# Two layers of attention and experts on one core: the second norm's factors spread by DMA

## The chip, the core and the metric

One core of a Trainium2 chip runs the whole program. Its engines run side by side and meet only at semaphores: TensorE (PE, with weight loads shown apart as PEld), VectorE (DVE), ScalarE (ACT), GpSimd (POOL), and SyncE (SP), whose queue issues nearly all transfers here. The metric is the device time of one execution in microseconds. A run's time is the median of several executions; the profile is of one execution.

## The reference

Two transformer layers on x of 16 x 256 tokens with 128 features, all in float32. Each layer adds to x an attention and a mixture of experts, both of a norm of x. What matters here is that the attention norms once more what was already normed:

```
xn = layernorm(x)                       # outer norm, no weights
x  = x + attention(xn, ln_w, ln_b, ...) + experts(xn, ...)

# inside the attention of either layer:
mu, var = mean(xn), mean((xn - mu)**2)
xh = (xn - mu) * rsqrt(var + 1e-5) * ln_w + ln_b
```

Since xn has mean 0, the second norm is a factor per token, r2 = (var(xn) + 1e-5)**-0.5, then a weight and a bias per feature. Layer 0 has 8-head local attention with rotary positions and 8 experts (2 per token); layer 1 has a gated attention unit and 32 experts (8 per token).

## The kernel before

**Tiling.** The 4096 tokens are cut into NG = 8 groups of G = 512. A group's rows lie as 128 partitions x 4 chunks x 128 features (token c*128 + p is at partition p, chunk c). Matmuls want features on the partitions, so rows are turned: `transposed` (L175) takes a PSUM bank and turns the four chunks by PE against `ident`. Turned tiles are 128 features x 512 tokens.

**Norms.** `moments` (L141) and `normalise` (L155) make xn on DVE, with a power on POOL; `again` (L163) makes r2, 128 x 4 (one factor per token), its last step a power on POOL (L169). Then there are two turned forms of each group: `xnT` of the rows xn themselves, for the routing and the experts, copied out of PSUM by ACT; and `xhT`, for the attention. For the latter `scaled` (L171) multiplies the four chunks by r2 on DVE (L173), `transposed` turns them on PE (L179), and one ACT activation takes the bank to SBUF with the weight as scale and the bias as bias, both one value per partition (L363 in layer 0, L794 in layer 1).

**Layer 0's attention** (L506 to L621) is a loop over s from -3 to 64, one step per pair of heads and sequence, eight steps a group; a step takes about 5 us. The order of PE, DVE, ACT and POOL is written out by hand (`manual_schedule`, L506). In one step, in this order: PE turns the softmax of step s (`turned0`, L465); ACT copies it out (L472) and takes the exponentials of step s + 2 (L442); DVE divides three quarters of step s + 1 (L451); then come pieces of other groups' routing (`pieces`), and the steps of `prepare` (L357); DVE multiplies what `there` holds (L407); PE and DVE make the scores of step s + 3 (L426, L432); ACT divides the last quarter of step s + 1 (L456), up to s + 1 = 48; PE attends (L482). `prepare(g)` has two parts: the scaling, in the step that `turned_rows` names, and the turn with the activation, at the first step of the group before (s = 8(g - 1)). Its result `xhTs` is read by `rotated` (L386, from the next step on) and `values` (L370). `rotated` also has ACT copy a tile to `here` and SP move it in four transfers to `there` (L399), 32 partitions over.

SP's queue is not in the hand-written order. The framework's scheduler places its instructions at build time; so the transfers that zero `x_rows` (L615), written one every second step, stand in the trace in bunches of nine.

**The experts of layer 0** (L706 to L735) follow, untouched by the change.

**Layer 1** (L950 to L994): after a written start only POOL's order is by hand; PE, DVE, ACT and SP are ordered by the scheduler. For each group the loop runs 17 pairs of expert matmuls (`pair`, L937, L939, L974) and, between them, the attention of this group (`gau`), the expert choice of the next (`route1`, from L798; its weights `w` are turned on PE at L186 as `wT_ps`, stored by SP at L194, and spread over the partitions as `bc`, L842), and the preparation of the next group, `finish0` (L747), whose eight pieces end with the scaling (L790) and the turn with the activation (L792 to L795). `xhTs[g]` is read by `gau(g)`, which starts at the first pair of the next group.

Of the kernel before, what the change touches and what calls it, by code (L numbers as in the profile page):

```python
# [11 lines left out]
F32 = mybir.dt.float32  # L12
# [3 lines left out]
ALU = mybir.AluOpType  # L16
# [3 lines left out]
P = 128  # L20
B, N, D = 16, 256, 128
T = B * N
G = 512
NG = T // G
NC = G // P
# [22 lines left out]
def two_layers(ctx: ExitStack, tc: tile.TileContext, a: dict, out: bass.AP):  # L48
    nc = tc.nc
# [6 lines left out]
    rows = ctx.enter_context(tc.tile_pool(name="rows", bufs=2, space=bass.MemoryType.DRAM))  # L56
# [72 lines left out]
    xn_all = w_a.tile([P, NG * NC, D], F32, tag="xn_all", name="xn_all")  # L129
    r2_all = const.tile([P, NG, NC], F32, tag="r2_all", name="r2_all")  # L130
# [32 lines left out]
    def again(r2, var, rs, name):  # L163

        ve = small.tile([P, NC], F32, tag="bve2", name=f"bve2_{name}")
        nc.vector.tensor_tensor(ve, rs, rs, ALU.mult)
        nc.vector.tensor_tensor(ve, ve, var, ALU.mult)
        nc.vector.tensor_scalar(ve, ve, EPS, None, ALU.add)
        nc.gpsimd.tensor_tensor(r2, ve, mhalf, ALU.pow)  # L169

    def scaled(dst, src, r2):  # L171
        for c in range(NC):
            nc.vector.tensor_scalar(dst[:, c, :], src[:, c, :], r2[:, c : c + 1], None, ALU.mult)  # L173

    def transposed(src, name):  # L175

        t = mm_tile(name)
        for c in range(NC):
            nc.tensor.transpose(t[:, c * P : (c + 1) * P], src[:, c, :], ident)  # L179
        return t  # L180
# [155 lines left out]
    yTs, xnTs = [], []  # L336
    with first as pa:
        wk = pa.enter_context(tc.tile_pool(name="wkA", bufs=2))
# [16 lines left out]
        xhTs0, vs, oTs, heads, yps = {}, {}, {}, {}, {}  # L355

        def prepare(g):  # L357
            xh = wk.tile([P, NC, D], F32, tag="xh", name=f"xh_{g}")
            scaled(xh, xn_all[:, g * NC : (g + 1) * NC, :], r2_all[:, g, :])
            yield  # L360
            t = transposed(xh, f"xhT_{g}")
            xhT = wk.tile([P, G], F32, tag="xhT", name=f"xhTs_{g}")
            nc.scalar.activation(xhT, t, AF.Identity, bias=col("ln_b"), scale=col("ln_g"))  # L363
            xhTs0[g] = xhT
            vs[g] = wk.tile([P, NC, 512], F32, tag="v", name=f"v_{g}")
            yield
# [139 lines left out]
        with tc.manual_schedule(engines={order.PE, order.DVE, order.Activation, order.Pool}):  # L506
            routing = {g: routed(g) for g in range(NG)}
            preparing = {g: prepare(g) for g in range(NG)}

            def step(gens, g, n=1):  # L510
                if 0 <= g < NG:
                    for _ in range(n):
                        next(gens[g], None)

            def drain(fs):
                for f in fs:
                    f()
                fs.clear()

            pieces = {}
            for g in range(NG):
                b = 5 * g - 12
                ranks = (b + 12, b + 13, b + 14)
                if g == 0:
                    at = (-3, -2, -1, 0, 1, 2)
                elif g == 1:
                    at = (-1, 0, 1, 2, 4, 5, 6)
                elif g == NG - 1:  # L530
                    at = (b, b + 1, b + 2, b + 3, b + 4, b + 5, b + 6, b + 9, b + 10, b + 11)
                else:
                    at = (b, b + 1, b + 2, b + 4, b + 6, b + 8, b + 9, *ranks)
                for n in at:
                    pieces.setdefault(n, []).append(g)
            turned_rows = {2: 7, 3: 12, 4: 22, 5: 27, 6: 37, 7: 47}

            step(routing, 0, 3)
            step(preparing, 0, 2)
            rotated(0)  # L540
            drain(later)
            rotated(1)
            near, far, sums = turning.pop(0)
            near()
            step(routing, 0)
            step(routing, 1, 3)
            far()
            sums()
            drain(later)
            wo, upper, steps, tiles, sw1, sw2, gtw, gtb, tieg = load_rest()  # L550
            turning[0].pop(0)()
            for s in range(-3, NS + 1):
                g, r = divmod(s, 8)
                if 0 <= s < NS:
                    tps = turned0(s, sc.pop(s)[0])
                drain(later)
                if 0 <= s < NS:
                    pTs[s] = evicted(s, tps)
                if 0 <= s + 2 < NS:
                    sms[s + 2] = exponentials(s + 2, *sc[s + 2])  # L560
                if turning and len(turning[0]) == 3:
                    turning[0].pop(0)()
                    far = sums = None
                else:
                    far, sums = turning.pop(0) if turning else (None, None)
                if 0 <= s + 1 < NS:
                    sm = sms.pop(s + 1)
                    divided(s + 1, sc[s + 1][0], sm)

                if s == -2:  # L570
                    step(preparing, 1)
                for n in pieces.get(s, ()):
                    step(routing, n)
                if r == 0:
                    step(preparing, g + 1)
                for n in turned_rows:
                    if turned_rows[n] == s:
                        step(preparing, n)
                if s == 35:
                    placing = places0(wk)  # L580
                if 35 <= s < 43:
                    next(placing)
                if far:
                    far()
                if s + 3 < NS:
                    sc[s + 3] = scores(s + 3)
                if sums:
                    sums()
                if 0 <= s + 1 < SHARED:
                    divided_last(sc[s + 1][0], sm)  # L590
                if s >= 1:
                    attended(s - 1, pTs.pop(s - 1))

                if s % 2 and 2 <= (s + 7) // 2 < NS // 2:
                    rotated((s + 7) // 2)
                if s < -1:
                    for c in range(2):
                        values(0, 2 * (s + 3) + c)
                if s < 0:
                    continue  # L600
                if 0 < g < NG and r in (0, 2):
                    project(g - 1, r // 2)
                if s == NS - 2:
                    project(NG - 1, 0)
                if r in (4, 6) and g + 1 < NG:
                    values(g + 1, r - 4)
                    values(g + 1, r - 3)
                if s == 2:
                    zero = w_a.tile([P, 2 * D], F32, tag="zero", name="zero")
                    nc.gpsimd.memset(zero, 0.0)  # L610
                    x_r0 = x_rows.rearrange("(t p c) d -> p t (c d)", p=P, c=2)

                if s >= 2 and s % 2 == 0 and s - 2 < NT0:
                    n = min(2, NT0 - (s - 2))
                    nc.sync.dma_start(  # L615
                        out=x_r0[:, s - 2 : s - 2 + n, :], in_=zero.unsqueeze(1).to_broadcast([P, n, 2 * D])
                    )
                if s >= 41:
                    for n in range(3 * (s - 41), min(3 * (s - 40), 2 * NG * NC)):
                        scatter0(n, paces[n % 3])  # L620
            project(NG - 1, 1)  # L621
# [21 lines left out]
    with ExitStack() as pb:  # L643
        wk = pb.enter_context(tc.tile_pool(name="wkB", bufs=2))
# [81 lines left out]
        for t in range(NT0 + at[-1]):  # L726
# [3 lines left out]
            if t % 3 == 0 and t // 3 < len(wanted):  # L730
                name, shape, src = wanted[t // 3]
# [11 lines left out]
    with ExitStack() as pc:  # L743
        wk = pc.enter_context(tc.tile_pool(name="wkC", bufs=2, reuse_waits="tile"))
        xn1Ts, xhTs, scs, spread_w = {}, {}, {}, {}

        def finish0(g):  # L747

            yg = wk.tile([P, NC * 2, D], F32, tag="yg", name=f"yg_{g}", bufs=1)
            for c in range(NC):  # L750
                for s in range(2):
                    nc.gpsimd.indirect_dma_start(  # L752
                        out=yg[:, 2 * c + s, :], out_offset=None, in_=y_rows,
# [6 lines left out]
            t = transposed(yTs[g].rearrange("p (c t) -> p c t", t=P), f"yt_{g}")  # L760
# [9 lines left out]
            xn = wk.tile([P, NC, D], F32, tag="xn", name=f"xn1_{g}")  # L770
            r2 = small.tile([P, NC], F32, tag="brs2", name=f"brs2_{g}")
            again(r2, *normalise(xn, xs[g], *moments(xs[g], f"c{g}")), f"d{g}")
            nc.gpsimd.tensor_tensor(xs[g], xs[g], xn, ALU.add)
            yield
            t = transposed(xn, f"xn1T_{g}")
            xnT = wk.tile([P, G], F32, tag="xn1T", name=f"xn1Ts_{g}")
            nc.scalar.copy(xnT, t)
# [7 lines left out]
            sc = wk.tile([P, NC, E1], F32, tag="sc", name=f"sc_{g}")  # L785
            nc.scalar.activation(sc.rearrange("p c e -> p (c e)"), gl[:, : NC * E1], AF.Sigmoid)
            scs[g] = sc
            yield
            xh = wk.tile([P, NC, D], F32, tag="xh", name=f"xh1_{g}")
            scaled(xh, xn, r2)  # L790
            yield
            t = transposed(xh, f"xh1T_{g}")  # L792
            xhT = wk.tile([P, G], F32, tag="xh1T", name=f"xh1Ts_{g}")
            nc.scalar.activation(xhT, t, AF.Identity, bias=col("ln_b1"), scale=col("ln_w1"))  # L794
            xhTs[g] = xhT  # L795
# [298 lines left out]
```

## Time and profile before

| what | value |
|---|---|
| median of 3 runs (lowest, highest) | 957.95 us (957.24, 962.34) |
| the profiled execution, whole | 944.71 us |
| its span, first to last instruction | 942.9 us |
| granted TensorE clock | 0.996 |
| layer 0's attention | to about 345 us |
| layer 0's experts | about 345 to 440 us |
| layer 1 | from about 440 us; one group 59.2 us |
| turns of the second norm on PE | 64, of which the change leaves 8 |

The span is that of one execution, on which all single durations were read; the median of the runs is 13 us above that execution's time. Busy time of an engine counts overlapped matmuls to their modelled end, so a full PE row says that PE is never without work, not that each listed nanosecond could be had back; the chain of work that ended last gives each instruction only the time that it adds. A line of the timeline has the start, the duration, the engine, the line, the operation, output and inputs with their shapes, a count of merged instructions, and in brackets the idle time before it and what ended it.

### The profile page before, as it was taken

What the parts mean: (1) busy time and instruction counts of PE and PEld (TensorE: products, weight loads), DVE (VectorE), ACT (ScalarE), POOL (GpSimd) and SP (SyncE); (2) the same over time, 40 slices, a digit from 0 to 9 for tenths busy, and PEclk for the clock granted to TensorE, in tenths of its full rate; (3) what the DMA queues carried; (4) which work ended last, traced back from release to release, by engine and by line L of the source; (5) the groups of instructions that cost most, each with busy time, mean ns of one, the idle gap of its engine ahead of it and who ended that gap; (6) DMA issues with size and microseconds to landing.
All of it is one profiled execution on the core that took longest, in us unless ns stands there. A gap on an engine that the chain in (4) does not pass through costs nothing.

```text
span 942.9 us, 13590 instructions
## 1 busy us (share of the span) xinstructions
PE 899.7 (95%) x3848; PEld 516.7 (55%) x3848; DVE 702.7 (75%) x2265; ACT 491.3 (52%) x1200; POOL 287.3 (30%) x251
## 2 busy tenths in 40 slices
PE   3899999999999998989999999999999999999997
PEld 2556666555555648986445454554545545455453
DVE  4999999899999923332687685886868868688653
ACT  1788989798798853434433422434224342243411
POOL 2343433323467630001525231252322522221200
PEclk9999999999999999999999999999999999999999
DMA  7171110010122137873161434214342243421430
GB/s 198 25 243 32 27 31 24 24 34 23 49 76 78 55 117 237 245 219 128 28 169 48 120 79 107 74 53 112 85 107 70 56 108 89 106 64 42 102 88 11
DMA packets 64922, 84.54 MB, mean 90 GB/s; under 512 B 10321, under 2 KB 40785, under 8 KB 64337
## 3 DMA queue, kind: packets, MB, share of 16 engines
q1 hardware_dynamic: 60320, 74.75, 29.5%
q0 software_dynamic: 4096, 8.40, 2.9%
q8 instruction: 31, 0.51, 0.2%
q10 hardware_dynamic: 432, 0.53, 0.2%
q14 instruction: 43, 0.34, 0.1%
HBM read 58.22 MB, written 17.04 MB: 80 GB/s over the span
## 4 chain that ended last, share of the span: by engine, by line
PE 63%; DVE 22%; DMA 6%; ACT 3%; issue 2%; SPq 2%; POOL 1%; DVEq 0%; ACTq 0%; POOLq 0%
PE u L939 11%; PE g L937 10%; PE z L974 9%; DVE p L432 4%; PE s L426 4%; PE o L482 3%; DVE p L451 3%; PE o L912 3%; DMA y_rows<-yt 3%; PE yr L696 2%; PE h L685 2%; PE t L465 2%; PE y L495 2%; PE z L992 2%; PE pq L386 2%
## 5 line engine op out<-in xcount | busy, mean ns | idle before, releaser
L941 ACT ACTIVATE h<-g 128x512 f32<-128x512 f32 x128 | 75.3, 594 | 232.0 <-PE g L937 225.6
L943 DVE TENSOR_TENSOR h<-h,u 128x512 f32<-128x512 f32 x128 | 87.2, 683 | 62.9 <-PE u L939 61.6
L937 PE MATMUL g<-xn1Ts,eg 128*128 128x512 f32 x256 | 131.4, 595 | 0.0
L939 PE MATMUL u<-xn1Ts,eu 128*128 128x512 f32 x256 | 130.2, 593 | 0.0
L442 ACT ACTIVATE p<-p,nm 128x256 f32<-128x256 f32 x256 | 127.5, 514 | 0.2 <-DVE nm L432 0.2
L974 PE MATMUL z<-h,ed 128*128 128x512 f32 x224 | 114.3, 593 | 0.0
L752 POOL DMA_INDIRECT yg<-y_rows,slot_at x64 | 69.8, 1090 | 121.4 <-PE hs L632 103.2
L432 DVE CUSTOM_DVE_ANT_0 p<-s,mask 128x256 f32<-128x256 f32 x256 | 92.7, 417 | 2.5 <-PE s L426 2.5
L946 DVE TENSOR_TENSOR h<-h,bc 128x512 f32<-128x512 f32 x128 | 90.2, 707 | 2.7
L426 PE MATMUL s<-k,q 64*128 64x256 f32 x512 | 84.5, 412 | 7.1 <-DVE k L411 4.3
L465 PEld LDWEIGHTS t<-ident,p 128*128 128x128 f32 x512 | 59.4, 140 | 35.0 <-issue 8.6
L322 POOL DMA_INDIRECT x_rows<-xn_all,slot_at x64 | 66.6, 1040 | 37.5 <-ACT pT L472 16.0
L939 PEld LDWEIGHTS u<-xn1Ts,eu 128*128 128x128 f32 x256 | 47.9, 192 | 54.4 <-issue 46.6
L472 ACT COPY pT<-t 128x512 f32<-128x512 f32 x128 | 69.2, 597 | 10.4 <-PE t L465 10.4
L974 PEld LDWEIGHTS z<-h,ed 128*128 128x128 f32 x224 | 42.4, 190 | 53.5 <-issue 45.6
L937 PEld LDWEIGHTS g<-xn1Ts,eg 128*128 128x128 f32 x256 | 46.3, 190 | 46.0 <-issue 41.1
L883 POOL TENSOR_TENSOR r1s<-r1s,sinr 128x512 f32<-128x512 f32 x16 | 23.5, 1468 | 156.9 <-ACT r1s L878 153.9
L482 PE MATMUL o<-pT,v 128*64 128x256 f32 x512 | 70.3, 396 | 0.3 <-ACT oT L487 0.2
L465 PE MATMUL t<-ident,p 128*128 128x128 f32 x512 | 67.3, 274 | 1.4 <-ACT p L456 1.4
L426 PEld LDWEIGHTS s<-k,q 64*128 64x128 f32 x512 | 51.2, 189 | 25.0 <-DVE nm L432 9.0
L451 DVE TENSOR_SCALAR p<-p,sm 128x256 f32<-128x256 f32 x208 | 62.0, 356 | 2.3
L688 ACT ACTIVATE h0s<-h,we 128x256 f32<-128x256 f32 x78 | 32.7, 470 | 57.6 <-issue 36.9
(252 smaller groups left out, 1541.3 us busy)
## 6 DMA issues: line engine op xcount, KB each, us to landing
bc<-rows_r SPq DMA_DIRECT2D x128, 256.0 KB, 4.2
there<-here SPq DMA_DIRECT2D x128, 64.0 KB, 2.0
we<-in_ex_dram SPq DMA_DIRECT2D x39, 129.0 KB, 3.2
xt<-x_rows SPq DMA_DIRECT2D x39, 128.0 KB, 3.2
y_rows<-yt SPq DMA_DIRECT2D x39, 128.0 KB, 3.0
x_rows<-zero SPq DMA_DIRECT2D x19, 256.0 KB, 3.3
x<-in_x_dram SPq DMA_DIRECT2D x8, 256.0 KB, 5.6
out_dram<-out SPq DMA_DIRECT2D x8, 256.0 KB, 2.6
```

What stands on the lines that cost most here:

```text
L426: nc.tensor.matmul(sp[h][:, i, :], q[rows, b, i * P : (i + 1) * P], k[rows, b, :], start=True, stop=True)
L432: nc.vector.tensor_tensor_reduce(out=pr[:, h, i, :], in0=sp[h][:, i, :], in1=mask[:, i, :], scale=-1.0, scalar=-NEG, op0=ALU.add, op1=ALU. ...
L442: paces[1] = nc.scalar.activation(row, row, AF.Exp, bias=nm[:, n : n + 1], scale=-1.0, accum_out=sm[:, n : n + 1])
L451: nc.vector.tensor_scalar(row, row, sm[:, n : n + 1], None, ALU.mult)
L465: nc.tensor.transpose(tp[:, at : at + P], pr[:, h, i, j * P : (j + 1) * P], ident)
L482: nc.tensor.matmul(op[h * DH : (h + 1) * DH, :], vs[g][:, 2 * b + j, (2 * hp + h) * DH : (2 * hp + h + 1) * DH], pT[:, h, j, :], start=(j ...
L937: nc.tensor.matmul(gp, wg, xn1Ts[g], start=True, stop=True)
L939: nc.tensor.matmul(up, wu, xn1Ts[g], start=True, stop=True)
L941: nc.scalar.activation(h, gp, AF.Silu)
L943: nc.vector.tensor_tensor(h, h, up, ALU.mult)
L946: nc.vector.tensor_tensor(h, h, spread_w[g][n // 2][:, n % 2, :], ALU.mult)
L974: nc.tensor.matmul(zp, w, r, start=(n == 1), stop=False)
```

## The change

In both layers the groups 1 to 7 no longer scale and turn the rows a second time. The factors r2 (128 x 4) are stored by SP to a row of 512 floats in DRAM (`row_stored`), and read back by SP onto all 128 partitions (`row_spread`, 128 x 512). DVE multiplies that tile in place by the turned rows that the routing has anyway (`xnTs[g]` in layer 0, `xnT` in layer 1), and the activation reads the product from SBUF. Group 0 stays as it was.

In layer 0 `prepare(g)` now has three parts. Store and spread come in the steps that `factors` names, the multiply and the activation where turn and activation were, at s = 8(g - 1). In layer 1 the store comes with the piece that turns xn, the spread with the routing scores, and the multiply with the activation in the last piece. The tile for the spread row takes the buffers of the scaled rows (tag `xh`, two of them).

```diff
+    def row_stored(r2, name):
+        d = rows.tile([1, G], F32, tag="row", name=f"row_{name}")
+        nc.sync.dma_start(out=d.rearrange("o (c p) -> p (o c)", p=P), in_=r2)
+        return d
+
+    def row_spread(d, pool, name):
+        t = pool.tile([P, G], F32, tag="xh", name=name)
+        nc.sync.dma_start(out=t, in_=d[0].partition_broadcast(P))
+        return t
...
         def prepare(g):
-            xh = wk.tile([P, NC, D], F32, tag="xh", name=f"xh_{g}")
-            scaled(xh, xn_all[:, g * NC : (g + 1) * NC, :], r2_all[:, g, :])
-            yield
-            t = transposed(xh, f"xhT_{g}")
+            if g:
+                d = row_stored(r2_all[:, g, :], f"a{g}")
+                yield
+                t = row_spread(d, wk, f"xh_{g}")
+                yield
+                nc.vector.tensor_tensor(t, t, xnTs[g], ALU.mult)
+            else:
+                xh = wk.tile([P, NC, D], F32, tag="xh", name=f"xh_{g}")
+                scaled(xh, xn_all[:, g * NC : (g + 1) * NC, :], r2_all[:, g, :])
+                yield
+                t = transposed(xh, f"xhT_{g}")
             xhT = wk.tile([P, G], F32, tag="xhT", name=f"xhTs_{g}")
             nc.scalar.activation(xhT, t, AF.Identity, bias=col("ln_b"), scale=col("ln_g"))
...
-            turned_rows = {2: 7, 3: 12, 4: 22, 5: 27, 6: 37, 7: 47}
+            factors = {1: (-3, -2), 2: (4, 6), 3: (10, 12), 4: (18, 20), 5: (27, 29), 6: (34, 36), 7: (43, 45)}
...
-                if s == -2:
-                    step(preparing, 1)
                 for n in pieces.get(s, ()):
                     step(routing, n)
                 if r == 0:
                     step(preparing, g + 1)
-                for n in turned_rows:
-                    if turned_rows[n] == s:
+                for n in factors:
+                    if s in factors[n]:
                         step(preparing, n)
...
         def finish0(g):
...
+            if g:
+                row = row_stored(r2, f"b{g}")
             t = transposed(xn, f"xn1T_{g}")
...
             scs[g] = sc
+            if g:
+                bc = row_spread(row, wk, f"xh1_{g}")
             yield
-            xh = wk.tile([P, NC, D], F32, tag="xh", name=f"xh1_{g}")
-            scaled(xh, xn, r2)
+            if not g:
+                xh = wk.tile([P, NC, D], F32, tag="xh", name=f"xh1_{g}")
+                scaled(xh, xn, r2)
             yield
-            t = transposed(xh, f"xh1T_{g}")
+            if g:
+                t = bc
+                nc.vector.tensor_tensor(t, t, xnT, ALU.mult)
+            else:
+                t = transposed(xh, f"xh1T_{g}")
             xhT = wk.tile([P, G], F32, tag="xh1T", name=f"xh1Ts_{g}")
             nc.scalar.activation(xhT, t, AF.Identity, bias=col("ln_b1"), scale=col("ln_w1"))
```

## Prediction, made before the changed kernel was run

> **What bounds the kernel now.** I read the page's busy line first, then the busy time by stage, then the chain of work that ended last, and last the timeline around the instructions that the change touches. The stages below are my cuts: two of layer 0's attention, one group of layer 1. Columns after the stretch: its length, then busy us and count of PE, PEld, DVE, ACT, POOL, then granted clock, DMA share, GB/s.
>
> ```profile
> PE 899.7 (95%) x3848; PEld 516.7 (55%) x3848; DVE 702.7 (75%) x2265; ACT 491.3 (52%) x1200; POOL 287.3 (30%) x251
> ...
> 67.00:121.00 54.00, 54.00 (x324) 33.26 (x325) 52.29 (x218) 48.72 (x150) 20.44 (x16) 1.00 0.15 38
> 229.00:320.00 91.00, 88.52 (x530) 52.08 (x528) 88.81 (x322) 77.88 (x241) 54.59 (x51) 1.00 0.22 63
> 579.00:638.00 59.00, 58.74 (x173) 29.89 (x172) 45.08 (x121) 21.04 (x32) 18.17 (x15) 1.00 0.34 86
> ```
>
> Two different machines are seen here. In layer 0's attention PE, DVE and ACT are all nearly full (97 to 100%, 97%, 86 to 90%), so whoever waits passes it on. In layer 1 PE alone is full and DVE has 14 us spare per group of 59. The chain says which engine sets the end where:
>
> ```profile
> 116.16 0.44 PE xhT L179 x4
> ...
> 148.88 0.78 DVE xh L173 x4
> ...
> 196.75 0.44 PE xhT L179 x4
> ```
> ```profile
> 565.35 0.44 PE xh1T L179 x4
> ```
>
> Going through the whole chain by time: DVE leads at 28 to 67, 126 to 167 and 236 to 320 us, PE leads at 67 to 121 and 167 to 229. In layer 1 it is PE, with one piece on DVE per group (567.6 to 572.8: the expert choice, which PE's turn of the weights `wT_ps` waits for). The page gives four turns 4 x 0.273 us busy, but the chain gives them 0.44: matmuls overlap, and 0.44 is what PE gets back.
>
> **What goes and what comes, per later group (7 in each layer).** Removed: four turns, 0.44 us of PE; four scalings of 128x128, 0.78 us of DVE. Added: one multiply 128x512 by 128x512. Its nearest row is the same shape from SBUF, `sq<-there,sinq`, 0.60 us from start to start (0.69 with its end). The activation reads SBUF instead of PSUM: 0.81 us (`r1s<-base`, 64x512, scale and bias) against 0.78, nothing. DVE thus gains 0.18 per group. Here a rule speaks against the change: the Trainium skill, "VectorE: DVE Perf Modes", section "Mode 2×_2P — use both read ports for one tensor", says that an f32 tensor-by-scalar handles two elements a cycle and a tensor-by-tensor one. At the page's 0.96 GHz, my estimate from it is 4 x 67 = 267 ns of streaming before and 533 after, a loss of 0.27 us a group, so 14 x 0.45 = 6.3 us more DVE work than by the rows. The rows decide, since each of the four short scalings takes 0.195 from start to start, far over 67 ns.
>
> **The two transfers.** The store writes 512 floats one by one to DRAM (partition p, column c goes to c*128+p); the spread reads 2 KB 128 times. Nearest rows:
>
> ```profile
> bc<-rows_r SPq DMA_DIRECT2D x128, 256.0 KB, 4.2
> rows_r<-wT SPq DMA_DIRECT2D x8, 64.0 KB, 1.6
> ```
>
> Spread: the same form as `bc`, 3.5 to 4.2 us, and `bc` go out in pairs, so I take 3.7. Store: the trace has no DRAM write of four-byte pieces. At least the 1.6 us of `rows_r`. Above, the Trainium skill, "DMA: Bandwidth & Descriptors": its rules for kernel authors say that a non-contiguous last dimension becomes one descriptor per element, and its section "Measured (HBM→SBUF, 128 partitions, SWDGE, issued from GpSimd)" gives some 10.5 ns a packet; 512 of these are an estimate of 5.4 us, 7.0 with the 1.6. No run here shows it. I take 2.3, near the row, since the pieces are spread over 16 engines. Factors to row: 2.3 + 0.1 + 3.7 = 6.1 us, at worst 11.2.
>
> Layer 0 covers that. Group 1 is tightest: its factors are ready at 20.7 and SP is free at 22.6, so the row lands at 28.7 (worst 33.8); the multiply stands at 41. For groups 2 to 7 four or more steps of 5 us lie between. On SP's queue stand the `there<-here` moves: in steady state the last of four lands some 2.5 us before `sq` reads it (130.7 against 133.16). Store and spread issue in about 0.45 us each, and SP can wait 2.3 between them: 3.2 at worst, once a group, so at most 0.7 us late. POOL's queue gets nothing new; SP's store waits for its power. Cost 0; without that cover up to 7 x 0.7 = 5 us.
>
> **What moves in layer 0: ACT now waits for DVE.** The scaling stood some steps ahead (s = 7, 12, 22, ...). The multiply stands in the step with s = 8k, behind that step's three divisions and a routing piece, and the activation in ACT's written order waits for it. PE's turn used to be done long before. Step 16 shows it:
>
> ```profile
> 118.22 0.88 DVE L451 TENSOR_SCALAR p<-p,sm 128x256 f32<-128x256 f32 x3
> 118.78 0.79 ACT L363 ACTIVATE xhTs<-xhT,vec 128x512 f32<-128x512 f32 x1
> 119.45 0.52 ACT L456 ACTIVATE p<-p,sm 128x256 f32<-128x256 f32 x1
> 120.25 0.19 DVE L231 TENSOR_TENSOR lg<-lg,rmx 128x32 f32<-128x32 f32 x1
> 120.36 0.42 DVE L432 CUSTOM_DVE_ANT_0 p<-s,mask 128x256 f32<-128x256 f32 x1
> 120.85 1.04 PE L465 MATMUL t<-ident,p 128*128 128x128 f32 x8
> 121.49 1.07 ACT L472 COPY pT<-t 128x512 f32<-128x512 f32 x2 [1.26 <-PE t L465]
> ```
>
> The multiply comes in at 120.36 and ends at 121.05; ACT stood ready at 118.78: a wait of 2.27. Behind it in ACT's queue is L456, which divides the last quarter of `p`, and PE's next eight turns (L465) wait for that quarter. The same reading for groups 1 to 7: multiply ends 41.99, 81.21, 121.05, 159.84, 201.45, 238.95, 280.26; ACT ready 40.17, 79.84, 118.78, 157.74, 199.38, 238.83, 278.69; waits 1.8, 1.4, 2.3, 2.1, 2.1, 0.1, 1.6, sum 11.4. Most is absorbed: ACT then idles 0.7 to 1.7 us for PE anyway (the 1.26 above), and where DVE leads it does not matter. Where PE leads, L456 now ends the turns later by more than the 0.44 saved: group 2, L456 ends 82.4 and the last three turns 82.8 against 82.2 (+0.6); group 3, 122.7 against 121.7, less 0.78 because DVE, almost never idle there, comes earlier by the removed scaling (+0.2); group 5, 203.1 against 201.9, less a 0.2 that PE waited anyway (+1.0). Where DVE leads: scalings out in groups 1, 4, 7 (-2.34), multiplies in 1, 4, 6, 7 (+2.40), and +0.2 in group 1, whose late ACT delays `here`. Layer 0: 0.6 + 0.2 + 1.0 + 0.06 + 0.2 = **+2.1 us**. Ends: -1.3 if ACT's wait costs nothing (3 x -0.44 + 0.06), about +10 if it is passed on in full (11.4 - 1.3).
>
> **Layer 1.** Here the framework's scheduler orders PE, DVE, ACT and SP; only POOL is written.
>
> ```profile
> 557.70 1.23 SPq L842 DMA_DIRECT2D bc<-rows_r  x2
> 557.83 1.01 POOL L169 TENSOR_TENSOR brs<-bve_d,mhalf 128x4 f32<-128x4 f32 x1 [2.66 <-DVE bve_d L168]
> 558.88 1.29 DVE L173 TENSOR_SCALAR xh<-xn,brs 128x128 f32<-128x128 f32 x1 [0.51 <-POOL brs L169]
> 567.61 0.69 DVE L943 TENSOR_TENSOR h<-h,u 128x512 f32<-128x512 f32 x1 [1.11 <-PE u L939]
> 572.89 0.61 PE L186 MATMUL wT_ps<-ident,w 128*32 128x128 f32 x4 [0.23 <-DVE w L834]
> ```
>
> Factors are ready at 558.84, and SP has issued its last `bc` by 558.93. The row lands at 558.9 + 6.1 = 565.0 (worst 570.1). DVE has a gap of 1.11 before 567.61, so a multiply at 565 to 567 is free and the group gains PE's 0.44. A multiply inside the expert choice delays `w` by 0.60 against 0.44 gained: +0.16. Nobody needs the activation before the next group begins, 20 us on. Between -0.44 and +0.16 I take -0.2, since the landing is nearer the gap: 7 x -0.2 = **-1.4 us** (ends -3.1 and +1.1). This rests on DVE not reaching the multiply before the row: then DVE stands still, the choice behind it, and PE at `wT_ps`.
>
> **Sum.** +2.1 - 1.4 = +0.7 us on the profiled execution, whose span is 942.9 and whole time 944.71: 945.4. The runs' median is 957.95, 13 us over that execution; the change of stages carries over, so **958.7 us**.
>
> **Rivals.** (1) The above, a wash, 0.50; its own range, from the two layers' nearer ends, 955 to 962. (2) PE's time comes out whole: -1.3 - 3.1 = -4.4, 953.6; 0.15. For it: PE leads for most of the span. Against: L456's place in ACT's queue. (3) Slower: the scheduler counts on an earlier row than the chip gives, DVE stands x us beyond its gap in each layer-1 group: 2.1 + 7 x (0.16 + x). It decides from x = 0.2, where the sum passes +4.8; with x = 1, 968.2; 0.22. For it: the store's price is unknown, and DVE takes instructions strictly in order; against: the 1.11 gap and the 20 us during which the multiply may come. (4) ACT's seven waits are passed on whole: +10 - 1.4, 966.5; 0.13. For it: PE, DVE and ACT are all near full; against: ACT's idle 0.7 to 1.7. That the turns don't go is no case: 56 disappear for certain.
>
> **How the numbers follow.** A measurement of this kernel tells about 0.5% (4.8 us) from no change. Faster: half of rival 2, 0.08. Slower: 0.19 of rival 3, 0.10 of rival 4, 0.03 of rival 1's upper edge, 0.32. Same 0.60. Range 953.5 (half of rival 2 lies under it) to 969 (the outer parts of 3 and 4, about 0.12, over it).
>
> **What would show it.** Right: 56 fewer turns; ACT's activation L363 waiting 1 to 2 us for DVE in groups 1 to 5 and 7; no DVE wait for the spread; layer 1's period 59.2 falling to about 59.0. Wrong: layer 1's period grows with DVE waiting on DMA before the multiply (rival 3); PE waits before L465 of over 1 us in most groups (rival 4); a store over 7 us; `sq` waiting for `there`.

## The result, and the profile after

The changed kernel takes 1030.99 us (median of 4 runs, 1029.51 to 1034.01) against 957.6 us for the kernel before, measured beside it: ratio 1.077, 95% interval 1.073 to 1.081. It is slower by 73 us; the prediction had 958.7, and 969.0 as the upper end of its range.

The page of the changed kernel, the lines of busy time, of granted clock (in 40 slices, 9 is 90% or more) and of the chain of work that ended last, and below them the last two of the kernel before:

```profile
PE 925.7 (90%) x3792; PEld 521.5 (51%) x3792; DVE 696.0 (68%) x2223; ACT 491.9 (48%) x1200; POOL 285.0 (28%) x251
...
PEclk8888999999999999999998989989989899899999
...
PE 50%; DMA 16%; DVE 16%; issue 8%; ACT 5%; SPq 4%; POOL 2%; DVEq 0%; ACTq 0%; POOLq 0%
```
```profile
PEclk9999999999999999999999999999999999999999
...
PE 63%; DVE 22%; DMA 6%; ACT 3%; issue 2%; SPq 2%; POOL 1%; DVEq 0%; ACTq 0%; POOLq 0%
```

The 56 turns are gone (3848 to 3792 matmuls), and DVE has 42 instructions fewer. Yet PE's busy time has grown by 26 us, because the clock is no longer full throughout: within its span the trace has 98 us at half clock, in 17 windows, where that of the kernel before has 7 us in 3. The chain, which was 63% PE and 6% DMA, is now half PE and 16% DMA. The same three stages as before, found by the same steps of the kernel, with the columns of the prediction:

```profile
75.30:139.90 64.60, 57.88 (x319) 33.95 (x315) 51.33 (x210) 48.35 (x148) 18.63 (x14) 0.92 0.20 44
248.50:345.50 97.00, 91.19 (x514) 52.64 (x515) 89.14 (x313) 77.95 (x239) 53.83 (x51) 0.98 0.20 58
622.50:690.50 68.00, 61.40 (x170) 30.56 (x169) 44.18 (x118) 20.96 (x32) 17.63 (x15) 0.95 0.37 79
```

The first stage was 54 us with PE at 100%, now it is 64.6 with PE at 90%. A group of layer 1 was 59, now it is 68. Something stops PE in both layers. In layer 1 the list of waits names it. Columns: who waited for whom, us in total, how often, longest:

```profile
POOL q L431 <- DVE sq L427: 101.3, 18, 11.7
DVE xh L818 <- DMA xh<-row_b: 54.7, 7, 8.9
...
ACT xh1Ts L822 <- DVE xh L818: 47.4, 7, 7.6
...
PE z L1002 <- DVE h L974: 37.0, 6, 6.6
...
DVE sq L427 <- DMA there<-here: 14.5, 7, 4.7
```

The multiply (L818) waits for the spread seven times, 7.8 us each; PE, which needs the gated products `h` that DVE makes behind it, waits six times for 6 us. The last line is layer 0: `sq` now waits for `there`, seven times, up to 4.7 us. The chain through one group of layer 1 has the prices (start, duration, what):

```profile
595.54 9.99 DMA row_b<-brs
605.53 0.02 SPq L180
605.55 0.03 issue
605.58 3.87 DMA xh<-row_b
609.45 0.02 issue
609.48 0.04 DVE xh L818
...
612.02 2.07 PE z L1002 x2
```

The store alone takes 10 us to land, the spread 3.87. The timeline of the same group, DVE and PE around the multiply:

```profile
601.11 0.19 DVE L835 TENSOR_TENSOR gs<-t 128x16 f32<-128x16 f32 x1
...
609.48 0.69 DVE L818 TENSOR_TENSOR xh<-xh,xn1Ts 128x512 f32<-128x512 f32 x1 [8.18 <-DMA xh<-row_b]
...
612.02 2.07 PE L1002 MATMUL z<-h,ed 128*128 128x512 f32 x2 [5.85 <-DVE h L974]
```

DVE stands for 8.18 us. The scheduler put the multiply directly behind the first part of the expert choice (`gs`, 601.30), 5.8 us after the store's issue. The two matmuls then take 2.07 us, where two of them took 1.02 before the stop: from 609.4 the granted clock is half, for 6.8 us, of which PE stands for 2.6 and works for 4.2. One such window comes with every stop of layer 1 (seven, 3.8 to 6.6 us long). In the mean of the seven groups PE stands for 5.8 us and then works for 4.8 us at half clock, which by my estimate, half of it, costs 2.4. Less what the edit gives back, that is the loss: the seven periods from the first pair of group 0 to that of group 7 are 472.6 us in sum, against 417.4, 7.9 more per group.

In layer 0 SP's queue shows it. SP's timeline at group 3's store, DVE's row for `sq`, and last the same four moves in the kernel before:

```profile
72.25 0.36 SPq L174 DMA_DIRECT2D row_a<-r_all  x1
72.65 0.51 SPq L634 DMA_DIRECT2D x_rows<-zero  x1
74.86 9.21 SPq L419 DMA_DIRECT2D there<-here  x4
84.16 0.53 SPq L180 DMA_DIRECT2D xh<-row_a  x1
```
```profile
85.61 0.69 DVE L427 TENSOR_TENSOR sq<-there,sinq 128x512 f32<-128x512 f32 x1 [4.74 <-DMA there<-here]
```
```profile
66.58 2.42 SPq L399 DMA_DIRECT2D there<-here  x4
```

Four `there` moves took 2.42 us to issue before; behind the store they take 9.21, and DVE waits. Layer 0's copies of the turned softmax come 4.9 us later at s = 2, 10.2 at s = 8, 18.9 at s = 16, and 19.5 at s = 42.

The chips of the four sets of experiments ran the kernel before in 955.9, 946.3, 946.9 and 963.7 us, so ratios are compared; and on the slower of them the last steps of layer 0, from s = 44 on, fall behind even in a kernel whose layer 0 is that of before (layer 1 alone: 0.9 us late at s = 42, 12.9 at s = 63; the 97 us of the second stage above have such steps in them), so that I read layer 0's loss at s = 42.

### The profile page after: what moved, and what is told of

It reads as the page before. It is cut to its first block, busy times and chain, and to the rows that moved or that the text cites. A ratio compares the mean times of both kernels' runs of the same rounds, so it can differ in the third digit from the quotient of the medians.

```text
span 1028.5 us, 13436 instructions
## 1 busy us (share of the span) xinstructions
PE 925.7 (90%) x3792; PEld 521.5 (51%) x3792; DVE 696.0 (68%) x2223; ACT 491.9 (48%) x1200; POOL 285.0 (28%) x251
## 4 chain that ended last, share of the span: by engine, by line
PE 50%; DMA 16%; DVE 16%; issue 8%; ACT 5%; SPq 4%; POOL 2%; DVEq 0%; ACTq 0%; POOLq 0%
DMA row_b<-brs 7%; PE z L1002 6%; PE g L965 5%; PE u L967 5%; PE s L446 5%; PE o L502 4%; DMA xh<-row_b 3%; PE t L485 3%; DMA y_rows<-yt 3%; PE pv L390 2%; PE yr L715 2%; PE y L515 2%; PE h L704 2%; DVE p L452 2%; PE z L948 2%
## 5 line engine op out<-in xcount | busy, mean ns | idle before, releaser
L1002 PE MATMUL z<-h,ed 128*128 128x512 f32 x224 | 120.6, 623 | 37.0 <-DVE h L974 37.0
L967 PE MATMUL u<-xn1Ts,eu 128*128 128x512 f32 x256 | 132.6, 602 | 0.0
L446 PE MATMUL s<-k,q 64*128 64x256 f32 x512 | 88.1, 425 | 15.3 <-DVE nm L452 9.0
L771 POOL DMA_INDIRECT yg<-y_rows,slot_at x64 | 66.1, 1033 | 123.1 <-PE hs L651 104.7
L485 PEld LDWEIGHTS t<-ident,p 128*128 128x128 f32 x512 | 60.2, 142 | 45.6 <-issue 15.7
L502 PE MATMUL o<-pT,v 128*64 128x256 f32 x512 | 74.0, 413 | 5.2 <-issue 2.8
L431 POOL TENSOR_TENSOR q<-q,sq 128x512 f32<-128x512 f32 x22 | 33.8, 1535 | 101.3 <-DVE sq L427 101.3
```

The costliest lines, as they stand in the source:

```text
L446: nc.tensor.matmul(sp[h][:, i, :], q[rows, b, i * P : (i + 1) * P], k[rows, b, :], start=True, stop=True)
L485: nc.tensor.transpose(tp[:, at : at + P], pr[:, h, i, j * P : (j + 1) * P], ident)
L502: nc.tensor.matmul(op[h * DH : (h + 1) * DH, :], vs[g][:, 2 * b + j, (2 * hp + h) * DH : (2 * hp + h + 1) * DH], pT[:, h, j, :], start=(j ...
L967: nc.tensor.matmul(up, wu, xn1Ts[g], start=True, stop=True)
L1002: nc.tensor.matmul(zp, w, r, start=(n == 1), stop=False)
```

## The experiments

Theory A: everything lost comes from the store landing far later than the 2.3 us of the prediction. Rival B: what costs is the rest of the change, above all ACT's seven waits for the multiply.

**No store.** The spread reads a row of an input that is there from the start:

```diff
-        d = rows.tile([1, G], F32, tag="row", name=f"row_{name}")
-        nc.sync.dma_start(out=d.rearrange("o (c p) -> p (o c)", p=P), in_=r2)
-        return d
+        return a["wqk"][0:1, :]
...
```

> The changed kernel without its store: the spread reads the first row of an input that is there from the start, so groups 1 to 7 of both layers are multiplied by a row that is not their factors, and their results are not the reference's. Spread, multiply and the activation's wait for the multiply stay. Theory A, the store lands 8 to 10 us after its issue and everything lost comes from waiting for it: 955 to 965 us, layer 1's period at 59 us, no wait of the multiply for the spread over 1 us. Rival B, the loss is in what stays (spread, multiply, the seven waits of ACT for DVE): 1015 us or more. Between them, 965 to 1015, both have a share.

954.79 us, ratio 0.9974 (0.9954 to 0.9995). The loss is gone, and the rest of the change is worth about -2.5 us. `xhTs` still waits five times for the multiply, 8.2 us in all (the longest 2.0), but layer 0 is only 0.3 us later at s = 42; layer 1's seven periods fall from 417.4 to 414.1. B is refuted.

**One layer at a time.** `prepare` with its steps, or `finish0`, is that of before; of the first, the line of the steps:

```diff
...
-            factors = {1: (-3, -2), 2: (4, 6), 3: (10, 12), 4: (18, 20), 5: (27, 29), 6: (34, 36), 7: (43, 45)}
+            turned_rows = {2: 7, 3: 12, 4: 22, 5: 27, 6: 37, 7: 47}
...
```

> The change in layer 0 alone; layer 1 keeps its scaling and second turn. By the two traces, in which the last step of layer 0's attention comes 32 us later, theory A (SP's queue stands still behind the spread that waits for the store, and the there moves behind it are late) gives 958 + 32 = 990 us, with layer 1's period back at 59.2. Rival: if layer 0's loss is nothing but a consequence of code that is shared or of the slower clock later on, 970 us or less. The prediction's own number for this half is 960.

> The change in layer 1 alone; layer 0 is that of the kernel before. Theory A (DVE stands at the multiply for some 8 us a group, and PE after it at half clock): seven groups of 66.7 to 68.5 us instead of 59.2 are 7 x 7.5 to 9 = 52 to 63 less what the last group hides, so 1000 to 1015 us. If the two halves add up to the whole loss of 73 us, this one is 958 + 73 - 32 = 999. Rival: a loss that needs both halves (together more than the sum) would leave this one under 980. The prediction's own number is 956.

Layer 0 alone: 975.99 us, ratio 1.0217 (1.0166 to 1.0268), +20 us; layer 1 alone: 1014.84, 1.0623 (1.057 to 1.0676), +59 us. The 32 us expected of layer 0 included the late steps that are no part of the change; at s = 42 this kernel is 15.7 us late. The two add up to 79 against the 73 of the whole, within the intervals.

**A store that nobody reads**, in the kernel before, at the steps where the change has it:

```diff
...
+                for n in stores:
+                    if stores[n] == s:
+                        row_stored(r2_all[:, n, :], f"a{n}")
...
+            if g:
+                row_stored(r2, f"b{g}")
             t = transposed(xn, f"xn1T_{g}")
```

> The kernel before, with all fourteen element-wise stores of the factors added at their places in SP's queue, and nobody who reads them. Theory A (what costs is the waiting for a late store, not the store itself): 957 to 965 us, with a store that still lands 8 to 10 us after its issue. Rival C (the 7168 four-byte writes hinder the other transfers or SP by themselves): 980 us or more.

971.03 us, ratio 1.0148 (1.0092 to 1.0203): between what the two expected, and the most instructive miss. Layer 1 lost nothing (seven periods of 418.1), but layer 0 is 12.9 us late at s = 42, most of the 15.7 of the change in layer 0 alone. So most of layer 0's loss is not SP waiting for the store on behalf of the spread, as theory A had it; nobody waits for this store. SP's and DVE's timelines behind the stores at 66.67 and 121.40:

```profile
66.67 0.36 SPq L174 DMA_DIRECT2D row_a<-r_all  x1
67.07 0.51 SPq L625 DMA_DIRECT2D x_rows<-zero  x1
67.69 6.11 SPq L405 DMA_DIRECT2D there<-here  x4
...
```
```profile
121.40 0.36 SPq L174 DMA_DIRECT2D row_a<-r_all  x1
121.94 12.33 SPq L405 DMA_DIRECT2D there<-here  x8
```
```profile
133.10 0.69 DVE L413 TENSOR_TENSOR sq<-there,sinq 128x512 f32<-128x512 f32 x1 [3.91 <-DMA there<-here]
```

From 67.69 on, one of the four issues takes 4.29 us instead of 0.59. At 121.94 four of the eight issue at once, without delay, by 124.35 (the other four at 131.86), and the packets in the trace are through by 125.5; yet `sq` has to wait. The trace also has the counts that a landing transfer adds to its semaphore, 16 each: the last one of this store comes at 132.28, 10.9 us after its issue, and the last ones of the four moves behind it, one after the other, at 132.45, 132.66, 132.81 and 132.97. The packets tell more: behind the store at 66.67 all 512 four-byte ones start within about a microsecond and take 7 to 9 ns each, and then fifteen packets of 1 and 2 KB take 0.8 to 8.2 us each, where such packets take 0.05 to 0.17. The store holds up the transfers behind it, in their issue, in their data or in their landing.

**The multiply later in layer 1.** DVE's order in layer 1 is the scheduler's, and whether writing the piece later would move the multiply there was not run alone. Here the piece is written later, and the multiply also gets one more operand, which is ready late:

```diff
+                    if n == 13:
+                        one[0] = small.tile([P, 1], F32, tag="one", name=f"one_{g}")
+                        nc.vector.tensor_scalar(one[0], queue[-1][1][:, 0:1], 0.0, 1.0, ALU.mult, ALU.add)
...
-                        for _ in range({4: 1, 5: 2, 7: 1, 8: 1, 9: 2}.get(n, 0)):
+                        for _ in range({4: 1, 5: 2, 7: 1, 8: 1, 9: 1, 13: 1}.get(n, 0)):
...
-                nc.vector.tensor_tensor(t, t, xnT, ALU.mult)
+                nc.vector.scalar_tensor_tensor(t, t, one[0], xnT, ALU.mult, ALU.mult)
```

> The changed kernel with its four-byte store, but in layer 1 the multiply reads one more operand, a column of ones made from the gated product of pair 13, so that the scheduler must put it some 30 DVE instructions (15 us) later, behind the whole expert choice. Theory A (layer 1 loses because DVE stands at a multiply that comes before the row): layer 1's groups return to 59.2 to 60 us, and what is left is layer 0's loss of 20 us: 974 to 982. Rival F (the store holds up other transfers of layer 1, and these are what PE waits for): 1000 or more. If ones cost more than they save, between 982 and 1000.

966.48 us, ratio 1.0207 (1.0161 to 1.0253), that is +20 us: all that is left is layer 0's loss. Layer 1's seven periods are 412.5, less than the 417.4 of the kernel before, though its stores land after 9.5 to 11.8 us. F is refuted: the late store costs layer 1 nothing once the multiply stands behind it.

**Fewer, larger pieces.** Each partition writes its four factors as one piece; the multiply then reads and writes the row with a stride of 16 bytes, and the activation reads it so (layer 0's multiply is shown):

```diff
-        nc.sync.dma_start(out=d.rearrange("o (c p) -> p (o c)", p=P), in_=r2)
+        nc.sync.dma_start(out=d.rearrange("o (p c) -> p (o c)", c=NC), in_=r2)
...
-                nc.vector.tensor_tensor(t, t, xnTs[g], ALU.mult)
+                t = t.rearrange("q (p c) -> q c p", c=NC)
+                nc.vector.tensor_tensor(t, t, xnTs[g].rearrange("q (c p) -> q c p", p=P), ALU.mult)
...
```

> The changed kernel with the row laid out so that each partition writes its four factors as one piece of 16 bytes (128 pieces in place of 512 of four bytes); multiply and activation read the row with a stride. Theory N (the store's price is its number of pieces): it lands 3 to 4 us after its issue, layer 1's wait of the multiply for the spread falls from 8 us to about 2, the time to 958 to 978. Rival R (any round trip by DRAM, whatever its pieces, takes 8 to 10 us): 1015 or more. A slower multiply or activation by the stride would show as their own durations, 0.69 and 0.81 us so far.

> Both edits together: 16-byte pieces and the late multiply of layer 1. Theory A with N: nothing waits for the row any more, 953 to 962 us, that is the time without a store (954.8) or the kernel before (955.9). If it stays above 966, the spread and the remaining pieces hold up other transfers.

The first, 16-byte pieces alone: 959.61 us, ratio 1.0116 (1.0064 to 1.0168). The timeline of one group of layer 1, store, spread and multiply:

```profile
568.77 0.54 SPq L174 DMA_DIRECT2D row_b<-brs  x1
572.75 0.33 SPq L180 DMA_DIRECT2D xh<-row_b  x1
576.97 1.10 DVE L820 TENSOR_TENSOR xh<-xh,xn1Ts 128x512 f32<-128x512 f32 x1 [2.45 <-DMA xh<-row_b]
```

The spread can now follow the store after 4.0 us (2.3 for group 1 of layer 0), and the multiply waits 2.45: R is refuted. With the late multiply as well: 948.62, ratio 1.0017 (0.9999 to 1.0035), as before. Here the stride has a price: the multiply takes 1.09 us instead of 0.69 and the activation 1.32 instead of 0.81. In layer 1 that is hidden (412.5 again); layer 0 is 7.6 us later at s = 42, and ACT waits in it for the slower multiply (11.8 us, seven times), so most of that is probably the stride's; no run separates the two.

**Where the pieces lie.** The unread stores again, each with 512 four-byte pieces, but with gaps between them:

```diff
-        d = rows.tile([1, G], F32, tag="row", name=f"row_{name}")
-        nc.sync.dma_start(out=d.rearrange("o (c p) -> p (o c)", p=P), in_=r2)
+        d = rows.tile([G, 16], F32, tag="far", name=f"row_{name}")
+        nc.sync.dma_start(out=d[:, 0:1].rearrange("(c p) o -> p (c o)", p=P), in_=r2)
```

> The kernel before with fourteen unread stores of 512 four-byte pieces, as in the run of the unread store (971 us), but the pieces lie 64 bytes apart in DRAM, where they lay side by side. Theory L (pieces that fall into the same stretch of memory hold each other up, and everything behind them): the packets behind the store no longer take microseconds, 955 to 962 us. Rival N (the number of pieces counts, wherever they go): 966 to 975.

> As the run with pieces 64 bytes apart (no difference from before, ratio 0.9991), but 32 bytes apart, so that two pieces share each 64 bytes. Theory L with a stretch of 64 bytes: about half of the pieces collide, the packets behind the store take microseconds again, ratio 1.005 to 1.02. Theory L with a stretch of 32 bytes or less: as before, 0.998 to 1.002.

> The unread stores once more, with the four-byte pieces 16 bytes apart, so that two of them share each 32 bytes (32 and 64 bytes apart cost nothing: ratios 0.9990 and 0.9991; side by side 1.0148). If the stretch in which pieces hold each other up is 32 bytes: the packets behind the store take microseconds in places, ratio 1.002 to 1.012. If it is 16 bytes or less, or only neighbours matter: 0.998 to 1.001.

64 bytes apart: ratio 0.9991 (0.9975 to 1.0007); 32 apart: 0.9990 (0.9975 to 1.0004); 16 apart: 1.0003 (0.9976 to 1.0030). None costs anything. SP's timeline of the first, at the same place:

```profile
66.61 0.36 SPq L174 DMA_DIRECT2D row_a<-r_all  x1
67.01 0.51 SPq L625 DMA_DIRECT2D x_rows<-zero  x1
67.63 2.42 SPq L405 DMA_DIRECT2D there<-here  x4
```

The four `there` issue in 2.42 us, as if there were no store, and in none of the three does a packet of 1 or 2 KB in the 12 us behind a store of layer 0 take over 0.46 us. By the semaphores' counts these stores land after 1.8 to 3.7 us in layer 0 and 3.5 to 5.0 in layer 1; those with pieces side by side, read or not, after 7.5 to 11.9 and 8.2 to 12.6. (Some counts are missing in the traces; where a spread waits for such a store I took the spread's issue, and the rest are left out.) So it is neither the number of pieces nor their size alone: 512 of four bytes cost nothing when spaced, and 128 of 16 bytes land early though they touch. It is 512 four-byte writes that lie side by side. The expectation of a shared stretch of 32 bytes fell with the last run. What happens between 4 and 16 bytes was not tried, and why the neighbours matter stays open. Nor was the changed kernel itself run with spaced pieces, which its spread would have to gather again.

**The change where it can pay**: layer 1 alone, with the late multiply and the four-byte store.

> The change in layer 1 alone, with its four-byte store and with the late multiply (operand from pair 13). In the run of the late multiply the seven periods of layer 1 were 412.5 us, 4.9 less than the 417.4 of the kernel before (7 x 0.44 for the turns is 3.1; the rest I can't account for yet). If this carries over with layer 0 untouched: ratio 0.993 to 0.997, so faster than both kernels. If layer 1's gain was owed to layer 0's later end: 0.998 to 1.002.

940.38 us, ratio 0.9923 (0.9898 to 0.9949): 7 us faster than the kernel before. Seven periods are 411.4 against 417.4. One group in the stages' view, and its row and weights in the timeline:

```profile
585.30:643.70 58.40, 58.37 (x170) 29.71 (x169) 44.42 (x118) 21.08 (x32) 17.64 (x15) 1.00 0.45 92
```
```profile
559.70 0.55 SPq L174 DMA_DIRECT2D row_b<-brs  x1
570.01 0.34 SPq L180 DMA_DIRECT2D xh<-row_b  x1
...
573.59 0.60 PE L198 MATMUL wT_ps<-ident,w 128*32 128x128 f32 x4
...
579.45 0.75 DVE L811 SCALAR_TENSOR_TENSOR xh<-xh,one,xn1Ts 128x512 f32<-128x512 f32 x1
```

The store takes 10.3 us here too, and the multiply comes 20 us after its issue without waiting. The gain per group is 0.86 us: 0.44 is PE's turns, and 0.23 to 0.25 the wait of `wT_ps` for `w`, which stood behind the scaling (1.5 us in six groups before, none now). The remaining 0.2 I can't assign.

## Why the prediction was wrong

- **"Store: I take 2.3, near the row."** This step failed. The store lands after 8.0 to 11.9 us in layer 0, and in layer 1 the spread behind it waits until 9.4 to 10.4. For the same pieces at 16 bytes' distance or more, the 2.3 would have been about right in layer 0 (1.8 to 3.7) and low in layer 1 (3.5 to 5.0). But `rows_r` moves pieces of 2 KB, and this store 512 neighbouring ones of four bytes; the higher end, 7.0 from the skill's price per packet, was nearer and still short, and not for its own reason: that price makes the 512 packets last 5.4 us, but they take 7 to 9 ns each and all start within about a microsecond. What takes the time comes after them.
- **"Factors to row 6.1 us, at worst 11.2."** Measured 13.9, of which the spread is 3.87 (taken at 3.7, right).
- **"DVE has a gap of 1.11 before 567.61, so a multiply at 565 to 567 is free."** The scheduler put the multiply behind `gs`, at a place that DVE reached 5.8 us after the store's issue, as if the row were there. This is rival 3, whose mechanism was right: DVE stands, and PE behind it. Its x was mis-sized: 1 us was tried, 8.18 is seen. Its own formula, 7 x (0.16 + 8.2), gives 58.5 for layer 1; layer 1 alone measured 59. That they agree is partly luck: PE stands for 5.8 us a group and not 8.2, and the half clock behind each stop, which was in no step of it, makes up 2.4 more. The Trainium skill, "TensorE: Matmul & The Clock Gate", Part 1, gives half rate after an idle window of about 3.4 us. Layer 1's stops of 3.8 to 6.6 us agree; but half clock also came where PE had stood for less, 1.2 us at 60.9 in the changed kernel and 1.8 at 165.3 in the one before, so here the measurement decides.
- **"Cost 0; without that cover up to 7 x 0.7 = 5 us"** for SP's queue. Measured 15.7 us by s = 42 with the change in layer 0 alone, and 12.9 for stores that nobody waits for. The step counted the wait on the queue and the issue time, and no effect of the store on transfers behind it. The Trainium skill has such an effect, in "DMA: Bandwidth & Descriptors", section "Back-pressure in remote DMA": stalled writes stall the same DMA engine's other queues. It says so of transfers between cores; this case's packets of up to 8.2 us look like it on one core, but all of them are of the store's own queue, and that its writes stall is not shown. Its "Specifications" put a read-modify-write under 512 bytes; by the spaced pieces small size alone costs nothing here.
- **ACT's seven waits, "mostly absorbed", +2.1 us.** Right in kind: without the store the five waits that remain sum to 8.2 us, and layer 0 is 0.3 us late at s = 42. Rival 4 is out. Of the prediction's four signs of being wrong, three came: DVE waiting for DMA before the multiply, a store over 7 us, and `sq` waiting for `there`.
- **The multiply at 0.69 by its row, against the rule on tensor-by-tensor f32.** The row held: 0.68 to 0.69.
- **Layer 1, -1.4 us.** With a row that is there in time -3.3 (no store), with the late multiply -4.9 and -6.0. The step counted the 0.44 of the turns, and not that `w` comes earlier by the removed scaling.
- **The sum +0.7 without a late row**: measured -2.5 (interval -4.4 to -0.5).

## What to carry to other kernels

Before a transfer of a form that the trace does not show is given the price of the nearest row, look at how its destination is cut: 512 four-byte pieces lying side by side in DRAM took 7.5 to 12.6 us here and held up other transfers, and a multiply that the scheduler had placed before the row's landing passed this on to PE. Where a late transfer has slack, make the order say so: an operand that is ready late, with the piece written later, moved the reader, and turned +59 us into -7. A stop of PE can also cost the clock behind it: in layer 1, 2.4 us on top of 5.8.

## What the runs showed of the hardware that was not expected

- 512 four-byte writes to neighbouring addresses landed after 7.5 to 12.6 us; 128 of 16 bytes to as many bytes (2 KB) after 1.4 to 5.4; 512 of four bytes at 16, 32 or 64 bytes' distance after 1.8 to 5.0, and the kernel took no longer for them.
- While such a store lands, other transfers' packets of 1 and 2 KB took up to 8.2 us instead of 0.05 to 0.17, one issue on SP took 4.29 us instead of 0.59, and moves whose packets were through by 125.5 counted as landed at 132.5 to 133.0.
- With a stride of 16 bytes in f32, a 128x512 multiply on DVE (one operand and the result strided) took 1.09 us instead of 0.69, and an activation on ACT (operand strided) 1.32 instead of 0.81.
- The granted clock was half behind stops of PE of 3.8 to 6.6 us, and also behind some as short as 1.2 and 1.8 us.
